# Class scales by one-hot products in four row tiles of the TensorE array, and issued ahead of single token tiles

## The chip, the cores and the metric

The kernel runs on one core of one Trainium2 chip. Its time is the device time of one execution in microseconds (us), as the median of several executions. The engines are TensorE (PE, matrix products), VectorE (DVE, element-wise work), ScalarE (ACT, activations and copies), GpSimd (POOL, indirect loads and a few element-wise steps) and SyncE (SP, which issues the plain DMAs of this kernel in one queue, in order). "PEld" in the profile is TensorE's loading of weights.

## The reference

The reference works on x of shape 2 x 2048 x 512, that is 4096 tokens of 512 channels. A modulated linear layer, a gated linear recurrence and a gated MLP come first, and their result is added to x. What the change touches is the part after these. There, each token is normalised and scaled and shifted by rows that its class ids choose:

```python
h = _ln(x, pw_g[pathway_ids], pw_b[pathway_ids])        # 500 classes
h = _ln(h, cp_g[compartment_ids], cp_b[compartment_ids])  # 5 classes
t = _ln(x, tm_g[time_steps], tm_b[time_steps])            # 5 classes
s = _ln(x, ms_g[scale_type], ms_b[scale_type])            # 2 of 3 classes
cat = concatenate([w0*h, w1*t, w2*m, w3*n, w4*r, w5*s])   # m, n, r: x plus a vector
y = _ln(silu(cat @ int_W1 + int_b1) @ int_W2 + int_b2, int_g, int_be)
```

y is then quantised to int8 for each token, multiplied with a quantised 512 x 512 matrix, and added to x. Inputs and outputs are float32.

## The kernel before, in words

The first stages (the modulated layer, the recurrence, the two up-projections of the MLP) run over four spans of 1024 tokens. They are followed by the down-projection `down`, also over four spans, whose products `dn_a`, `dn_b` and `dn_d` read four operands b11, b12, b21 and b22 (tiles `op`), loaded from a DRAM scratch (line 701, `op<-pp_d`). A product is made by a scheme of seven smaller products ("steps") of sums and differences of these four (line 200 makes the sums on DVE). The dictionary `early` hangs small pieces of preparation behind these steps; in the first span they are the loading of the class tables (`load_classes`, lines 921 and 922), the making of one-hot rows (`one_hots`, line 899), the splitting of each class table into three bf16 parts (`split`, `class_gains`, lines 908 to 911), and loads of state weights (`load_state`, line 59). A later piece loads `rhsT` (line 59).

The last stage, the token stage, runs over eight blocks of 512 tokens, each as four token tiles of 128. For block i+1:

- `by_tokens` transposes x to tokens, normalises it, and gathers the pathway rows. It also transposes the one-hot rows of the four token tiles (line 1182, tile `tr_oh`), and ACT copies the result into `oh` (line 1186): 30 rows by 512 tokens.
- `by_channels` transposes the normalised tokens back to channels (line 1133) as `lnT` and `hT`; ACT copies them out (line 1136).
- `gains` multiplies them by the class scales. A scale for 128 channels and 512 tokens is one bf16 product of a 30-row table (10 classes in three bf16 parts) with the 30 one-hot rows (line 1224). Three tables (n = 0, 1, 2) and four groups of 128 channels make twelve products per block, in six pairs. Each pair fills one PSUM tile of two banks, named `gain`, out of two such tiles that all `tr` users share, and one DVE multiply (line 1228) consumes it, giving `tT`, `lnT` or `hT`.
- `up` is the first MLP product (`ps_h`, line 130), on block i, with `by_tokens` and `by_channels` of block i+1 and the int8 product of block i-1 as pieces among its steps. `added` (line 1264) adds the class shifts (table 3) in it.
- `down2` is the second MLP product of block i (`ps_o`, line 1300), one 512-wide product for each token tile, followed by a DVE addition (line 1304) and the statistics of the last norm (line 1110). It takes the token tiles in the order 2, 3, 0, 1.

A tile framework puts the instructions of each engine in an order of its own, from priorities and dependencies; the program above gives the data flow and a first order. In the order that it built, the six pairs of gains of block i+1 stand among the first products of `down2` of block i, two gains and then one ps_o product.

Of the kernel before, what the change touches and what calls it, by code (L numbers as in the profile page):

```python
# [9 lines left out]
FP = mybir.dt.float32  # L10
# [19 lines left out]
G = 32  # L30
# [20 lines left out]
def adaln_attn_ffn(ctx: ExitStack, tc: tile.TileContext, a: dict, out: bass.AP):  # L51
# [235 lines left out]


    groups = ident.rearrange("p (j r) -> p j r", r=G)
    sums = const.tile([P, G], FP, name="sums")  # L290
    nc.vector.tensor_reduce(sums, groups.rearrange("p j r -> p r j"), AX.X, ALU.add)
    apart = const.tile([P, 3, B], FP, name="apart")
    nc.vector.tensor_copy(apart, groups[:, 0:3, 0:B])
    nc.vector.tensor_add(apart[:, 0, :], groups[:, 0, 0:B], groups[:, 3, 0:B])
# [39 lines left out]
        wsq.append(t)  # L334
    rows_k = tp.tile([P, T], FP, tag="k", name="ps_dcoef_k")
    rows_of("ps_dcoef", [(st2[:, c, :], wsq[c]) for c in range(C)], rows_k)
    ps = columns_of("ps_dcoef", rows_k, sums[:, 0:B])
    dflat = dcoef.rearrange("p c b -> p (c b)")
    dv = small.tile([P, 2, C * B], FP, name="dv")
    nc.vector.tensor_scalar(  # L340
# [328 lines left out]


    R = 10
    onehot = w3.tile([P, NT, 3, R], BF, name="onehot", bufs=1)
    tables = w3.tile([3 * R, 4, D], BF, name="tables", bufs=1)
    idx_pw = w3.tile([P, NT], mybir.dt.int32, name="idx_pw", bufs=1)
    betas = w3.tile([P, 3, C, R], FP, name="betas", bufs=1)
    dn = ph1.enter_context(ExitStack())
# [131 lines left out]
    def state_columns(m):  # L808
        name = ("mem", "noi", "res")[m]
        v = vs[m]  # L810
        ps = columns_of(f"ps_sv_{m}", held[m][:, C, :], sums[:, 0:B])
        for o in range(C):
            nc.vector.tensor_scalar(
                v[:, o, :], ps[:, o, :], col(f"L0_cond2_{name}_b2", o), None, ALU.add
            )
# [67 lines left out]
    def one_hots():  # L883

        nc.sync.dma_start(idx_pw, a["idx_pw"])
        row_of = small.tile([P, R], FP, name="row_of")
        for k in range(R):
            nc.vector.memset(row_of[:, k : k + 1], float(k - (0 if k < 5 else 5 if k < 8 else 8)))
        ids = small.tile([P, 3, NT], FP, name="ids")
        for k, n in enumerate(("idx_c", "idx_m")):  # L890
            raw = small.tile([P, NT], mybir.dt.int32, tag="raw", name=n)
            nc.sync.dma_start(raw, a[n])
            nc.vector.tensor_copy(ids[:, k, :], raw)
        nc.vector.memset(ids[:, 2, : NT // 2], 0.0)
        nc.vector.memset(ids[:, 2, NT // 2 :], 1.0)
        for k, (lo, hi) in enumerate(((0, 5), (5, 8), (8, 10))):
            shape = [P, NT, hi - lo]
            for n in range(3):
                nc.vector.tensor_tensor(
                    onehot[:, :, n, lo:hi],  # L900
                    ids[:, k, :].unsqueeze(2).to_broadcast(shape),
                    row_of[:, lo:hi].unsqueeze(1).to_broadcast(shape), ALU.is_equal,
                )

    def split(k, t, parts, engine=nc.vector):

        for n, h in enumerate(parts):
            ins = engine.tensor_copy(h, t)
            if n < 2:
                engine.tensor_sub(t, t, h)  # L910
            nc.sync.dma_start(tables[n * R : n * R + R, k, :], h)
        return ins

    TABLES = (("tm", 0, 5), ("ms", 5, 3), ("cp", 0, 5))
# [189 lines left out]
    def tr(name, dtype=FP):  # L1104
        turn[0] ^= 1
        return tr_ps[turn[0]].tile([P, 2, D], dtype, tag="tr", name=name)
# [34 lines left out]
    def block(tag, i=None):  # L1141
        return place(tag if i is None else f"{tag}{i % 2}", C, T)
# [15 lines left out]
    def by_tokens(i, k, behind=()):  # L1158


        def queued(n):
            return tc.issue_after(behind[n].ins) if behind else nullcontext()

        x2n = k["x2n"] = place(f"x2n{i % 2}", J, D)
        mv = small.tile([P, J, 2], FP, tag="mv", name=f"mv1_{i}", bufs=4)
        for q in PAIRS:
            if behind:
                turn[0] = 1
            with queued(q):
                pt = tr(f"tr_x_{i}_{q}")  # L1170
                for j in (0, 1):
                    for c in range(C):
                        nc.tensor.transpose(
                            pt[:, j, ts(c, P)], k["x2T"][:, c, ts(2 * q + j, P)], ident
                        )
            nc.scalar.copy(duo(x2n, q), pt)
            for j in (2 * q, 2 * q + 1):
                stats(mv, j, x2n[:, j, :], f"s1_{i}")
        with queued(2):
            po = tr(f"tr_oh_{i}", BF)[: 3 * R].rearrange("r a b -> r (a b)")[:, :T]  # L1180
            for j in range(J):
                nc.tensor.transpose(
                    po[:, ts(j, P)], onehot[:, i * J + j].rearrange("p n r -> p (n r)"), identb
                )
        k["oh"] = place(f"oh{i % 2}", T, dtype=BF)[: 3 * R]
        nc.scalar.copy(k["oh"], po)
        r = rstd_of(mv, f"r1_{i}")

        h0 = k["h0"] = []
        mv2 = small.tile([P, J, 2], FP, tag="mv", name=f"mv2_{i}", bufs=4)  # L1190

        ln = k["ln"] = [place(f"o4_{q}", 2, D) for q in PAIRS]
        for q in PAIRS:
            pw = place(f"pw{q}", 2, 2 * D)
            h0.append(pw[:, :, 0:D])
            for j in (0, 1):
                gather(i * J + 2 * q + j, pw[:, j, :])
                normed(ln[q][:, j, :], x2n[:, 2 * q + j, :], mv, r, 2 * q + j)
            nc.vector.tensor_mul(h0[q], ln[q], h0[q])
            nc.vector.tensor_add(h0[q], h0[q], pw[:, :, D : 2 * D])  # L1200
            for j in (0, 1):
                stats(mv2, 2 * q + j, h0[q][:, j, :], f"s2_{i}")
        r = rstd_of(mv2, f"r2_{i}")
        for j in range(J):
            t = h0[j // 2][:, j % 2, :]
            last = normed(t, t, mv2, r, j)
        return last
# [5 lines left out]
        for q in PAIRS:  # L1213
            to_channels(hT, q, k["h0"][q], f"tr_h_{i}_{q}")

    def gains(i, k):

        tT = k["tT"] = block("tT")
        lnT, hT = k["lnT"], k["hT"]
        for n, dst, src in ((0, tT, lnT), (1, lnT, lnT), (2, hT, hT)):  # L1220
            for q in PAIRS:
                ps = tr(f"gain_{i}_{n}_{q}")
                for c in (0, 1):
                    nc.tensor.matmul(
                        ps[:, c, :], tables[:, n, ts(2 * q + c, P)], k["oh"],
                        start=True, stop=True,
                    )
                nc.vector.tensor_mul(duo(dst, q), ps, duo(src, q))

    h1s, o4s, mvs = {}, {}, {}  # L1230

# [2 lines left out]
    def up(i, k, then):  # L1234
# [25 lines left out]
        def added(n, ps):  # L1260

            o, half = {1: (0, h_a), 2: (0, h_b), 3: (2, h_b), 4: (2, h_a)}[n]
            for u in (0, 1):
                nc.tensor.matmul(
                    ps[u], tables[:, 3, ts(o + u, P)], k["oh"][:, half],
                    start=False, stop=(n != 2), skip_group_check=True,
                )

# [19 lines left out]
            banks, tap, out11, out12, out21, out22, then, added, True,  # L1288
        )

    def down2(i, then=()):

        h1 = h1s.pop(i)
        o4 = o4s[i] = [place(f"o4_{q}", 2, D) for q in PAIRS]
        mv = mvs[i] = small.tile([P, J, 2], FP, tag="mv", name=f"mv3_{i}", bufs=4)
        for q in (1, 0):
            for j in (2 * q, 2 * q + 1):
                ps = m2_ps.tile([P, D], FP, tag="mm", name=f"ps_o_{i}_{j}")
                for c in range(C):
                    nc.tensor.matmul(  # L1300
                        ps, h1[:, c, ts(j, P)], w2[:, c, :], start=(c == 0), stop=(c == C - 1)
                    )
                t = o4[q][:, j % 2, :]
                nc.vector.tensor_add(t, ps, b2_bc)
                stats(mv, j, t, f"s3_{i}")
            if q in then:
                then[q]()
# [57 lines left out]
    pb = m2_ps.tile([P, D], FP, tag="mm", name="ps_bias")[:R]  # L1365
    pc = m2_ps.tile([P, D], FP, tag="mm", name="ps_bias_s")[:R]
    n = 0
    nc.tensor.matmul(pb, sums[:, 0:R], bias, start=True, stop=False)
    for m, at in ((0, 0), (2, 2)):
        for c in range(C):  # L1370
            nc.tensor.matmul(
# [15 lines left out]
        nc.vector.tensor_sub(bias[:, 2 * P :], bias[:, 2 * P :], pc[:, 2 * P :])  # L1387
        tables_done = split(3, bias, [place(f"tab{n % 2}", D, dtype=BF)[:R] for n in range(3)], nc.gpsimd)
    by_channels(0, k)
    gains(0, k)  # L1390
    last = None
    for i in range(NB):
        nxt = load(i + 1) if i + 1 < NB else None
        then = {}
        if last:
            qs = []
            then[0] = lambda: qs.append(last_norm(i - 1))
            then[2] = lambda: int8_product(i - 1, qs[0], last["x2n"])
        if nxt:
            then[3] = lambda: by_tokens(i + 1, nxt)  # L1400
            then[6] = lambda: by_channels(i + 1, nxt)
        up(i, k, then)
        if nxt:
            gains(i + 1, nxt)
            down2(i)
        else:
            qs = {}

            def norm_of(q):
                qs[q] = last_norm(i, (q,))  # L1410
            down2(i, {1: lambda: norm_of(1)})
            int8_product(i, qs[1], k["x2n"], (1,))
            norm_of(0)
            int8_product(i, qs[0], k["x2n"], (0,))
        last, k = k, nxt
# [68 lines left out]
```

## The time and the profile before

| | us |
|---|---|
| median of 3 executions | 2105.15 |
| lowest and highest | 2104.56, 2105.45 |
| the profiled execution | 2105.82 |
| its span in the trace | 2104.0 |
| one block of the token stage, first gain to first gain | 78.95 |

Over the span PE is busy for 97%, DVE for 58%, ACT for 33% and POOL for 7%. The trace has a line for every instruction: start, length, engine, line of the program, operation, output and inputs, the size of the operands, and what ended an idle time before it. In such rows "x2" is a count of like instructions in a row, and the length goes from the first start to the last end. A product in float32 shows as two passes. Starts and ends are in us from the start of the span.

### The profile page before, as it was taken

The numbers are of one execution on the slowest core, as the hardware profiler recorded it, in microseconds if no ns is written. First come the engines' busy times: TensorE is split into PE (matmuls) and PEld (weight loads), VectorE is DVE, ScalarE is ACT, GpSimd is POOL, SyncE is SP. The second block draws the span as 40 slices with busy tenths as digits, with TensorE's granted clock in tenths as the row PEclk, the third lists the DMA queues.
The fourth block names the chain that finished last, engine by engine and source line by source line (L and its number), as shares of the span: only waits on it lengthen the run. The fifth ranks groups of instructions, "written<-read, shape, count | busy, mean of one in ns | idle before, by whom it ended". The sixth has DMA issues, their size and how long they took to land.

```text
span 2104.0 us, 16699 instructions
## 1 busy us (share of the span) xinstructions
PE 2048.2 (97%) x6230; PEld 1075.1 (51%) x6238; DVE 1213.3 (58%) x1788; ACT 691.5 (33%) x894; POOL 155.6 (7%) x125
## 2 busy tenths in 40 slices
PE   8989999999899999999999999999999999999996
PEld 4334444443344444444444444435776776776773
DVE  6875655565732433324335465486587787787765
ACT  3557787877542222222221000001312312312300
POOL 1240000001200000000000000072000000000000
PEclk9999999999999999999999999999999999999998
DMA  5672212132311212211235846624101201201000
GB/s 203 252 253 73 80 40 80 40 100 80 120 40 50 80 40 72 79 40 50 95 105 185 296 138 206 224 86 156 61 20 61 81 21 61 81 21 60 21 20 20
DMA packets 85071, 199.52 MB, mean 95 GB/s; under 512 B 6407, under 2 KB 34303, under 8 KB 80893
## 3 DMA queue, kind: packets, MB, share of 16 engines
q1 hardware_dynamic: 80380, 181.67, 25.1%
q0 software_dynamic: 4608, 16.78, 2.4%
q8 instruction: 49, 0.80, 0.2%
q14 instruction: 34, 0.27, 0.0%
HBM read 131.18 MB, written 67.13 MB: 94 GB/s over the span
## 4 chain that ended last, share of the span: by engine, by line
PE 85%; DVE 6%; ACT 6%; DMA 1%; issue 1%; SPq 0%; DVEq 0%; ACTq 0%
PE up_a L130 16%; PE ps_h_a L130 11%; PE up_d L130 8%; PE dn_a L130 7%; PE ps_o L1300 5%; PE ps_h_d L130 5%; PE rec_a L130 5%; PE up_b L130 4%; PE dn_d L130 4%; PE rec_d L130 4%; PE ps_h_b L130 3%; PE y_a L130 2%; PE rec_b L130 2%; PE dn_b L130 1%; PE ps_f L1347 1%
## 5 line engine op out<-in xcount | busy, mean ns | idle before, releaser
L130 PE MATMUL up_a<-h,w_up 128*128 128x512 f32 x384 | 172.8, 592 | 0.0
L130 PE MATMUL up_a<-h2T,w_up 128*128 128x512 f32 x384 | 172.6, 592 | 0.0
L130 PE MATMUL dn_a<-op,w_dn 128*128 128x512 f32 x384 | 167.4, 594 | 0.0
L623 DVE SCALAR_TENSOR_TENSOR prod<-up_d,cols,k 128x512 f32<-128x512 f32 x48 | 35.9, 751 | 198.4 <-ACT k L256 198.4
L256 ACT COPY k<-up_a 128x512 f32<-128x512 f32 x144 | 84.3, 585 | 197.7 <-PE up_a L130 197.6
L603 ACT ACTIVATE gate<-gate,cols 128x512 f32<-128x512 f32 x96 | 68.8, 721 | 213.4 <-DVE gate L602 213.4
L130 PE MATMUL rec_a<-hT,w_rec 128*128 128x512 f32 x256 | 116.7, 596 | 5.2 <-ACT k L256 5.2
L1300 PE MATMUL ps_o<-int_w,h 128*128 128x512 f32 x256 | 121.6, 610 | 0.0
L130 PEld LDWEIGHTS up_a<-h2T,w_up 128*128 128x128 f32 x384 | 73.0, 190 | 91.8 <-issue 91.8
L130 PEld LDWEIGHTS up_a<-h,w_up 128*128 128x128 f32 x384 | 72.9, 190 | 91.9 <-issue 89.4
L130 PE MATMUL rec_a<-h,w_rec 128*128 128x512 f32 x256 | 117.0, 596 | 1.6 <-ACT k L256 1.3
L130 PEld LDWEIGHTS dn_a<-op,w_dn 128*128 128x128 f32 x384 | 72.2, 190 | 88.8 <-issue 86.7
L130 PE MATMUL up_d<-h,w_up 128*128 128x512 f32 x192 | 86.4, 593 | 0.8 <-DVE prod L623 0.8
L130 PE MATMUL up_d<-h2T,w_up 128*128 128x512 f32 x192 | 87.0, 592 | 0.0
L130 PE MATMUL up_b<-h,w_up 128*128 128x512 f32 x192 | 86.3, 592 | 0.0
L130 PE MATMUL dn_d<-op,w_dn 128*128 128x512 f32 x192 | 84.2, 595 | 0.0
L130 PEld LDWEIGHTS rec_a<-hT,w_rec 128*128 128x128 f32 x256 | 47.9, 190 | 69.2 <-issue 55.0
L130 PEld LDWEIGHTS rec_a<-h,w_rec 128*128 128x128 f32 x256 | 48.7, 191 | 64.8 <-issue 59.7
L602 DVE TENSOR_TENSOR gate<-up_b,k 128x512 f32<-128x512 f32 x48 | 32.8, 690 | 73.1 <-PE up_b L130 72.1
L1300 PEld LDWEIGHTS ps_o<-int_w,h 128*128 128x128 f32 x256 | 45.0, 189 | 58.4 <-issue 58.4
L256 ACT COPY k<-rec_a 128x512 f32<-128x512 f32 x96 | 53.8, 580 | 51.7 <-PE rec_a L130 51.6
L130 PE MATMUL rec_d<-h,w_rec 128*128 128x512 f32 x128 | 60.6, 617 | 6.8 <-DVE i L534 5.3
(372 smaller groups left out, 3472.5 us busy)
## 6 DMA issues: line engine op xcount, KB each, us to landing
pp_d<-prod SPq DMA_DIRECT2D x48, 512.0 KB
op<-pp_d SPq DMA_DIRECT2D x16, 1536.0 KB
x<-in_xT SPq DMA_DIRECT2D x4, 2048.0 KB
y_d<-y SPq DMA_DIRECT2D x16, 512.0 KB
h_d<-y SPq DMA_DIRECT2D x16, 512.0 KB
h<-h_d SPq DMA_DIRECT2D x4, 2048.0 KB
yr<-y_d SPq DMA_DIRECT2D x16, 512.0 KB
hs_d<-yr SPq DMA_DIRECT2D x16, 512.0 KB
```

Of the source, the lines that this page charges most:

```text
L130: ins = nc.tensor.matmul(ps, ws[k // 2][:, slot, k % 2, ts(u, P)], xs[k], start=(first and k == 0), stop=(last and k == n - 1), skip_group ...
L256: nc.scalar.copy(t, ps)
L602: nc.vector.tensor_add(gate[u][:, half], ps, kept)
L603: nc.scalar.activation(gate[u][:, half], gate[u][:, half], AF.Gelu, bias=col("L0_attn_mlp_gate_b", fs[u]),)
L623: nc.vector.scalar_tensor_tensor(prod[u][:, b_], ps, col("L0_attn_mlp_fc_b", fs[u]), kept, ALU.add, ALU.add)
L1300: nc.tensor.matmul(ps, h1[:, c, ts(j, P)], w2[:, c, :], start=(c == 0), stop=(c == C - 1))
L1347: nc.tensor.matmul(ps, qT[:, j, ts(c, P)], rq[:, c, :], start=(c == 0), stop=(c == C - 1))
```

## The change

The one-hot rows get 32 columns instead of 30 (the two more are zero), and four copies of them are made by transposing each token tile four times, into partitions 0, 32, 64 and 96 of the PSUM tile. The three scale tables are likewise stored four times, at partitions 0, 32, 64 and 96; the table of shifts (number 3) is stored once. The four products of one table then read four different groups of 32 partitions, one for each group of 128 channels, and write four different PSUM banks. `gains` handles one table (n) for each call, and the calls for block i+1 stand in `down2` of block i, ahead of the token tiles 2, 3 and 0, instead of ahead of all of `down2`. One tile `ids` has a single buffer, and a tile is renamed (`sums` to `summing`), without other effect.

```diff
-    onehot = w3.tile([P, NT, 3, R], BF, name="onehot", bufs=1)
-    tables = w3.tile([3 * R, 4, D], BF, name="tables", bufs=1)
+    onehot = w3.tile([P, NT, G], BF, name="onehot", bufs=1)
+    tables = w3.tile([P, 4, D], BF, name="tables", bufs=1)
...
+        nc.gpsimd.memset(onehot, 0.0)
...
-                    onehot[:, :, n, lo:hi],
+                    onehot[:, :, n * R + lo : n * R + hi],
...
-            nc.sync.dma_start(tables[n * R : n * R + R, k, :], h)
+            for g in range(4 if k < 3 else 1):
+                nc.sync.dma_start(tables[G * g + n * R : G * g + n * R + R, k, :], h)
...
-            po = tr(f"tr_oh_{i}", BF)[: 3 * R].rearrange("r a b -> r (a b)")[:, :T]
+            po = tr(f"tr_oh_{i}", BF).rearrange("r a b -> r (a b)")[:, :T]
             for j in range(J):
-                nc.tensor.transpose(
-                    po[:, ts(j, P)], onehot[:, i * J + j].rearrange("p n r -> p (n r)"), identb
-                )
-        k["oh"] = place(f"oh{i % 2}", T, dtype=BF)[: 3 * R]
+                for g in range(4):
+                    nc.tensor.transpose(po[ts(g, G), ts(j, P)], onehot[:, i * J + j], identb)
+        k["oh"] = place(f"oh{i % 2}", T, dtype=BF)
...
-    def gains(i, k):
-
-        tT = k["tT"] = block("tT")
+    def gains(i, k, n):
         lnT, hT = k["lnT"], k["hT"]
-        for n, dst, src in ((0, tT, lnT), (1, lnT, lnT), (2, hT, hT)):
-            for q in PAIRS:
-                ps = tr(f"gain_{i}_{n}_{q}")
-                for c in (0, 1):
-                    nc.tensor.matmul(
-                        ps[:, c, :], tables[:, n, ts(2 * q + c, P)], k["oh"],
-                        start=True, stop=True,
-                    )
-                nc.vector.tensor_mul(duo(dst, q), ps, duo(src, q))
+        if n == 0:
+            k["tT"] = block("tT")
+        dst, src = ((k["tT"], lnT), (lnT, lnT), (hT, hT))[n]
+        ps = [tr(f"gain_{i}_{n}_{q}") for q in PAIRS]
+        for c in range(C):
+            of = slice(G * c, G * c + 3 * R)
+            nc.tensor.matmul(
+                ps[c // 2][:, c % 2, :], tables[of, n, ts(c, P)], k["oh"][of],
+                start=True, stop=True,
+            )
+        for q in PAIRS:
+            nc.vector.tensor_mul(duo(dst, q), ps[q], duo(src, q))
...
-    def down2(i, then=()):
+    def down2(i, nxt=None, then=()):
...
             for j in (2 * q, 2 * q + 1):
+                if nxt and j in (2, 3, 0):
+                    gains(i + 1, nxt, (2, 3, 0).index(j))
                 ps = m2_ps.tile([P, D], FP, tag="mm", name=f"ps_o_{i}_{j}")
...
-    gains(0, k)
+    for n in range(3):
+        gains(0, k, n)
...
-            gains(i + 1, nxt)
-            down2(i)
+            down2(i, nxt)
```

Here P is 128, G is 32, R is 10, C and J are 4, D and T are 512, and NT is 32, the number of token tiles.

More of the change, by code (lines that the diff above doesn't have):

```diff
@@ L289, in adaln_attn_ffn @@
     groups = ident.rearrange("p (j r) -> p j r", r=G)
-    sums = const.tile([P, G], FP, name="sums")
-    nc.vector.tensor_reduce(sums, groups.rearrange("p j r -> p r j"), AX.X, ALU.add)
+    summing = const.tile([P, G], FP, name="sums")
+    nc.vector.tensor_reduce(summing, groups.rearrange("p j r -> p r j"), AX.X, ALU.add)
     apart = const.tile([P, 3, B], FP, name="apart")
@@ L336, in adaln_attn_ffn @@
     rows_of("ps_dcoef", [(st2[:, c, :], wsq[c]) for c in range(C)], rows_k)
-    ps = columns_of("ps_dcoef", rows_k, sums[:, 0:B])
+    ps = columns_of("ps_dcoef", rows_k, summing[:, 0:B])
     dflat = dcoef.rearrange("p c b -> p (c b)")
@@ L810, in state_columns @@
         v = vs[m]
-        ps = columns_of(f"ps_sv_{m}", held[m][:, C, :], sums[:, 0:B])
+        ps = columns_of(f"ps_sv_{m}", held[m][:, C, :], summing[:, 0:B])
         for o in range(C):
@@ L888, in one_hots @@
             nc.vector.memset(row_of[:, k : k + 1], float(k - (0 if k < 5 else 5 if k < 8 else 8)))
-        ids = small.tile([P, 3, NT], FP, name="ids")
+        ids = small.tile([P, 3, NT], FP, name="ids", bufs=1)
         for k, n in enumerate(("idx_c", "idx_m")):
@@ L1264, in added @@
                 nc.tensor.matmul(
-                    ps[u], tables[:, 3, ts(o + u, P)], k["oh"][:, half],
+                    ps[u], tables[: 3 * R, 3, ts(o + u, P)], k["oh"][: 3 * R, half],
                     start=False, stop=(n != 2), skip_group_check=True,
@@ L1367, in adaln_attn_ffn @@
     n = 0
-    nc.tensor.matmul(pb, sums[:, 0:R], bias, start=True, stop=False)
+    nc.tensor.matmul(pb, summing[:, 0:R], bias, start=True, stop=False)
     for m, at in ((0, 0), (2, 2)):
@@ L1410, in norm_of @@
                 qs[q] = last_norm(i, (q,))
-            down2(i, {1: lambda: norm_of(1)})
+            down2(i, None, {1: lambda: norm_of(1)})
             int8_product(i, qs[1], k["x2n"], (1,))
```

## The prediction

> **What bounds the kernel now.** I read the page's busy line first, then windows, timeline and tile views of the token stage, then waits. The profiled execution took 2105.82 us (span 2104.0, clock 0.992), 0.67 above the median 2105.15; sums are made against it, and 0.67 comes off at the end. A measurement of this kernel can tell about 0.2% (4.2 us) from no change.
>
> ```profile
> PE 2048.2 (97%) x6230; PEld 1075.1 (51%) x6238; DVE 1213.3 (58%) x1788; ACT 691.5 (33%) x894; POOL 155.6 (7%) x125
> ...
> 1593.54:1672.49 78.95, 78.82 (x360) 56.78 (x360) 59.53 (x99) 16.64 (x24) 3.76 (x5) 1.00 0.15 54
> ```
>
> The second line is one token block, gain to gain: 78.95 us, TensorE (PE) busy 78.82, VectorE (DVE) 59.53. So PE sets a block, and what leaves PE's row leaves the block. The PE timeline where the change acts:
>
> ```profile
> 1593.54 0.60 PE L1224 MATMUL gain<-zone_C,tables 30*128 30x512 bf16 x2
> 1594.07 1.13 PE L1300 MATMUL ps_o<-int_w,h 128*128 128x512 f32 x2
> 1595.13 0.60 PE L1224 MATMUL gain<-zone_C,tables 30*128 30x512 bf16 x2
> 1595.66 1.12 PE L1300 MATMUL ps_o<-int_w,h 128*128 128x512 f32 x2
> ...
> 1601.48 0.60 PE L1224 MATMUL gain<-zone_C,tables 30*128 30x512 bf16 x2
> 1602.02 9.71 PE L1300 MATMUL ps_o<-int_w,h 128*128 128x512 f32 x22
> ```
>
> Columns: start, length, instructions. Six pairs of gains, 1.59 us apart (1595.13 − 1593.54), each followed by two passes of ps_o. A pass alone takes (9.71 − 0.59)/21 = 0.434, with 0.59 the length of a single one. So **one pair costs PE 1.59 − 2 × 0.43 = 0.73 us**. The single starts in the trace divide it: 0.226 between the two gains, and about 0.50 that a pair pays however many gains it has: 0.304 from its last gain to ps_o, 0.105 extra on the next pass (0.534 for 0.429), 0.09 extra before the next pair.
>
> [...] column tiles run together:
>
> ```profile
> 1166.78 1.06 PE L301 MATMUL ps_sh_r<-state_w 128*32 128x512 f32 x8
> ```
>
> Eight 512-column passes in 1.06 us; one by one they would need 8 × 0.43 = 3.4. Row tiles do not occur before. [...] Four gains at 0.226 are 0.90[...]; perfect overlap gives 0.23. [...] the change's four outputs go to the two banks each of two tr tiles.
>
> **The change, part by part.**
>
> *Gains of blocks 1 to 7.* The built order has, where six pairs stood: pair, one ps_o, pair, three ps_o, four gains (n=1), four ps_o, four gains (n=2), eight ps_o. Two gains that overlap cost 0.73 − 0.22 = 0.51; four cost 0.50 + 0.02 = 0.52[...]. Before 6 × 0.73 = 4.38; after 2 × 0.51 + 2 × 0.52 = 2.06. **−2.3 per block, −16.1 in seven**[...].
>
> *Block 0* keeps six groups, each now overlapping: 6 × 0.2 = **−1.2** (bounds −0.3, if waits for DVE's multiplies fill the room, to −1.3).
>
> *Do the products come in time?* A gain waits for its tr tile. Before, DVE multiplies (1.22 each) follow gains 1.59 apart; now PE is at group three 0.51 + 0.86 + 0.51 + 2.58 = 4.46 after the first, at group four 4.46 + 0.52 + 3.44 = 8.42. ACT's second hT copy ends at 1594.65, 1.11 after the first gain, ahead of the second pair (1.37). Group three needs the tT products, done near 3.3. Group four needs both lnT products; DVE's built order puts a ps_o add and a bn_stats among them. From the last pass of tile 2, 4.65 + 0.59 + 1.15 + 0.7 + 1.22 = 8.3 (starts of such rows in DVE's timeline). Slack of 0.1 only, and 0.5 late is the bound, 3.5 in seven blocks: I take **+0.5** in all.
>
> *Transposes of the one-hot rows*, 4 to 16 per block.
>
> ```profile
> 1568.81 0.40 PE L1182 MATMUL tr_oh<-identb,onehot 128*30 128x128 bf16 x4
> 1569.14 0.70 PE L130 MATMUL ps_h_a<-tT,w_int 128*128 128x256 f32 x2
> ```
>
> Four cost 0.33 to the next start, 0.055 apart. Twelve more, in column tiles like ps_sh_r's, add about 0.05; one by one 12 × 0.055 = 0.66. **+0.4** in eight blocks (0 to +5.3). The ACT copy goes from 30 to 128 partitions with the same 512 elements each, so its 0.57 stays, under an ACT busy 16.6 of 79.
>
> *Table copies.* Nine DMA issues of SP become 36.
>
> ```profile
> L911 SPq DMA_DIRECT2D tables<-classes x9: 722/743/835, 1154.8 to 1176.9; - x9
> ```
>
> 27 × 0.743 = 20 us on SP, between 1155 and 1197 us in the down stage. Behind them wait loads of op and the state weights; behind DVE's 4 us of waits on such landings (three, now on four copies each) stand taps and operand sums. I walked the built SP order with the old times: op b11 leaves about 4 us later (1174), b12 about 1191, and b21, which PE reads next, at 1202.2, since its buffer is read by PE until 1200.7 and SP had idle room till then.
>
> ```profile
> 1202.04 0.61 SPq L701 DMA_DIRECT2D op<-pp_d  x1
> ...
> PE dn_b L130 <- DMA op<-pp_d: 1.4, 1, 1.4
> ```
>
> This b21 load is the one PE waits for (1.4). Two 1 MB loads, state_w and rhsT, issued at 1186.85 and 1197.86, now stand behind it in SP's order, so it shares the DMA engines with less: **−0.7** (between −1.4 and +2). On DVE the operand sum op_21 (1163.2) has one of the longer waits ahead of it, and the taps that follow wait for PE themselves until 1179, 1184 and 1195, up to 2 us each: covered. rhsT, later by about 10, is reduced ahead of a sum that PE needs at 1247, ready near 1237.
>
> *Rest.* The memset of onehot on POOL (a 128x1024 f32 one takes 0.95) falls at 1128, where POOL is otherwise idle, before DVE's is_equal; DVE's next big sum waits for PE till 1136: nothing. Renamed tiles, table 3 and the two `added` products: as before.
>
> Sum: −16.1 − 1.2 + 0.5 + 0.4 − 0.7 = −17.1; 2105.8 − 17.1 = 2088.7 profiled, less 0.67: **2088.0**.
>
> **The rivals.**
>
> *A. Row tiles run one after another.* For it: the trace before shows column tiles only. Against it: the independence shown there[...]. Pairs keep 0.73, fours cost 0.50 + 3 × 0.226 = 1.18: 3.82 for 4.38, −0.56 × 7 = −3.9; block 0 nothing. With transposes in a row (+5.3) and −0.7: 2105.15 + 0.7 = about **2106**, with quick transposes 2101: no change that can be told.
>
> *B. DVE is late at the last four* by its bound, 0.5 in seven blocks: 2088 + 3 = **2091**. Speaks for it: slack 0.1. Against: no wait beyond DVE's own row.
>
> *C. Slower: SP's queue becomes the wait.* If SP had no idle room ahead of b21, its issue would come 20 us late, and PE would stand in the dn_b row for as much. Some copies also wait for DVE, which overwrites their source only once the fourth copy has landed, 3 × 0.74 = 2.2 after the first. Without relief the rest of the sum is −16.4: 2105.15 − 16.4 + 20 + 2.2 = **2111**. It decides once b21 leaves over 16.4 us later than at 1202. For it: 27 copies in front. Against it: the queue's rows between 1155 and 1202 sum to 19 of 47 us, so 20 more can be held, and b21 waits for PE anyway.
>
> **How the numbers follow.** Forecast 0.80 (with sizes from 2085.5 to 2091), B 0.09, A or half of it 0.06, C 0.03, other 0.02. Lower end: 2105.15 − 16.1 − 1.3 − 1.4 = 2086.3[...]: 2085. Upper end: B, serial transposes (+4.9) and no relief (+0.7) give 2096.6: 2096.5. Faster takes forecast, B and a little of A; same the rest of A and a C half held; slower the remainder of C.
>
> **What would show it.** Right: the block period falls from 78.95 to about 76.7 with PE still over 99% busy; L1228 gains in groups of two, two, four, four, with starts within 0.02 us; 16 transposes in under 0.45; no PE wait on a product lnT. Wrong: gains 0.22 apart in a group (A); a PE wait ahead of the last group (B); a longer wait in the row dn_b from op (C), or DVE taps late after 1161; a period that falls with a gap between groups above 0.55.

## The result, and the profile after

The change makes the kernel faster by 0.9%: 2085.93 us (2084.65 to 2088.27) against 2105.3 us, a ratio of 0.9909 with a 95% interval of 0.9891 to 0.9926. The forecast was 2088.0. A second set of runs gave 2088.38 and 0.9913 (0.9898 to 0.9928). The profiled execution after took 2084.65 us, with a span of 2082.9.

One block of the token stage, first gain to first gain, in the windows view of after (period, then busy time and instructions of PE, PEld, DVE, ACT, POOL):

```profile
1586.13:1662.79 76.66, 76.58 (x375) 56.70 (x374) 59.03 (x99) 16.66 (x24) 3.75 (x5) 1.00 0.16 56
```

The period falls from 78.95 to 76.66, that is by 2.29, and PE is still busy for 99.9% of it. The PE timeline of after, at the place that was shown of before:

```profile
1586.13 0.39 PE L1228 MATMUL gain<-zone_C,tables 30*128 30x512 bf16 x2
1586.44 1.12 PE L1308 MATMUL ps_o<-int_w,h 128*128 128x512 f32 x2
1587.50 0.39 PE L1228 MATMUL gain<-zone_C,tables 30*128 30x512 bf16 x2
1587.82 2.84 PE L1308 MATMUL ps_o<-int_w,h 128*128 128x512 f32 x6
1590.59 0.40 PE L1228 MATMUL gain<-zone_C,tables 30*128 30x512 bf16 x4
1590.92 3.70 PE L1308 MATMUL ps_o<-int_w,h 128*128 128x512 f32 x8
1594.55 0.39 PE L1228 MATMUL gain<-zone_C,tables 30*128 30x512 bf16 x4
```

A row of four gains takes 0.40, as long as a row of two (0.39), and hardly longer than one gain (0.384 in the tile view): the four run together. Their single starts in the trace are 3 to 4 ns apart. The distance to the next ps_o is 0.32 for two and 0.33 for four.

DVE's rows ahead of the last group show how near the products came to being late (start, length, in brackets the idle time before and what ended it):

```profile
1590.70 0.69 DVE L1312 TENSOR_TENSOR zone_C<-ps_o,rows 128x512 f32<-128x512 f32 x1 [1.54 <-PE ps_o L1308]
1591.31 1.21 DVE L1233 TENSOR_TENSOR lnT<-gain,lnT 128x1024 f32<-128x1024 f32 x1
1592.44 0.68 DVE L1113 BATCH_NORM_STATS2 s_st<-zone_C 128x6 f32<-128x512 f32 x1
1593.04 1.21 DVE L1233 TENSOR_TENSOR lnT<-gain,lnT 128x1024 f32<-128x1024 f32 x1
```

The second lnT product ends at 1594.25, and the last group starts at 1594.55 without a wait: a slack of 0.3.

The transposes of the one-hot rows, sixteen instead of four:

```profile
1434.43 0.41 PE L1186 MATMUL tr_oh<-identb,onehot 128*32 128x128 bf16 x16
1434.76 0.66 PE L1136 MATMUL tr_l<-ident,zone_A 128*128 128x128 f32 x4
```

They take 0.33 to the next start, as four did before (unrounded, 0.01 more). The table copies and the wait behind them (the tile view, then the waits):

```profile
L914 SPq DMA_DIRECT2D tables<-classes x36: 706/708/1478, 1151.6 to 1193.2; - x36
...
  DVE classes L910: 10.3, 3
```

```profile
PE dn_b L130 <- DMA op<-pp_d: 0.5, 1, 0.5
```

DVE waits 10.3 us for landings in place of 4.0, and PE's wait for b21 is 0.5 in place of 1.4.

The two traces differ by 2104.0 − 2082.9 = 21.1 us. From the first gain to the end it is 649.05 before and 632.16 after, −16.9. The other 4.2 lie ahead of the first gain, and 2.7 of them ahead of the recurrence, in a part that the change does not touch. The experiments show where most of these 4.2 come from.

### The profile page after: what moved, and what is told of

Same layout as the page of the kernel before. It is cut to its first block, busy times and chain, and to the rows that moved or that the text cites. A ratio compares the mean times of both kernels' runs of the same rounds, so it can differ in the third digit from the quotient of the medians.

```text
span 2082.9 us, 16921 instructions
## 1 busy us (share of the span) xinstructions
PE 2029.6 (97%) x6334; PEld 1072.6 (51%) x6334; DVE 1208.1 (58%) x1788; ACT 691.3 (33%) x894; POOL 154.1 (7%) x126
## 4 chain that ended last, share of the span: by engine, by line
PE 82%; DVE 7%; ACT 6%; DMA 3%; issue 1%; SPq 1%; DVEq 0%; ACTq 0%
PE up_a L130 16%; PE ps_h_a L130 11%; PE up_d L130 8%; PE ps_h_d L130 5%; PE ps_o L1308 5%; PE rec_a L130 5%; PE dn_a L130 5%; PE up_b L130 4%; PE rec_d L130 4%; PE dn_d L130 3%; PE ps_h_b L130 3%; PE y_a L130 2%; PE rec_b L130 2%; PE ps_f L1355 2%; PE y_d L130 1%
```

## The experiments

The theory, from the prediction: a group of gains costs PE g = 0.51 us however many run together in it, and each gain on rows that are already in use adds s = 0.22. (A row tile is here one of the four groups of 32 partitions of the change, used by a product on 30 rows; a serial step is a gain that follows another on the same rows.) The rivals were that tiling alone or placement alone carries the gain, and that the copies cost something that a larger gain hides.

### The change once more

Edit: none.

> The changed kernel once more, unedited, as the base for the other kernels here and for the scatter of the start. In its first profile y_a, the first product of the first stage, stood 2.3 us earlier than in the profile of before, ahead of anything that the change touches. Theory: this is scatter between executions (how long the first products run at half pace); then it moves again here by about 1 to 2 us and the time is 2085 to 2088. Rival: the change itself brings it (its program is laid out differently); then y_a starts again near 18.6 us for its second half, as in the first profile after.

Measured: 2088.38 us (ratio 0.9913), span 2086.6. Period and token stage are those of the first profile (76.66; 632.16 from the first gain to the end). The start is not. The timelines of PE's second product of the first stage, here and in the first profile after:

```profile
21.17 3.60 PE L130 MATMUL y_b<-x,w_cond 128*128 128x512 f32 x8
```

```profile
18.61 3.60 PE L130 MATMUL y_b<-x,w_cond 128*128 128x512 f32 x8
```

In some executions the first products run at half pace for longer (starts 0.85 apart in place of 0.43). In the twelve profiles y_b starts between 18.6 and 22.6, and two profiles of one kernel lie 2.6 apart here and 2.2 for the kernel before. The start is scatter, not the change.

### Placement alone

```diff
-            for g in range(4 if k < 3 else 1):
+            for g in range(1):
...
-                for g in range(4):
+                for g in range(1):
...
-            of = slice(G * c, G * c + 3 * R)
+            of = slice(0, 3 * R)
```

> Placement alone: gains called ahead of token tiles 2, 3 and 0 as in the change, but all on one group of 32 partitions, with one copy of tables and one-hot rows. Theory (a group costs 0.50 us however many gains it has, and gains on the same rows cost 0.226 each): groups of 2, 2, 4, 4, that is 2 x 0.73 + 2 x 1.18 = 3.82 for 4.38 us per block, -0.56 x 7 = -3.9 against before, nothing in block 0 or in the down stage: 2101.4. Rival, that the saving is the placement's: close to 2089, the change's own time. Rival, that DVE becomes late at the last group since four products in a row delay it: 2103 to 2105.

Measured: 2100.93 us, ratio 0.9978 (0.9967 to 0.9988).

```profile
1593.43:1671.78 78.35, 78.27 (x361) 57.11 (x361) 59.03 (x99) 16.63 (x24) 3.74 (x5) 1.00 0.16 54
```

The period is 78.35, −0.60 where −0.56 was expected. Four gains of one group on one set of rows stand at 0.96 to the next ps_o, where four in row tiles take 0.33. Placement alone is a quarter of the change's 2.29.

### Row tiles alone

```diff
-                if nxt and j in (2, 3, 0):
-                    gains(i + 1, nxt, (2, 3, 0).index(j))
...
-            down2(i, nxt)
+            for n in range(3):
+                gains(i + 1, nxt, n)
+            down2(i)
```

> Row tiles alone: tables and one-hot rows in four groups as in the change, but all gains of a block ahead of down2, as before. Theory: six groups of two that overlap, 0.51 for 0.73 us: -0.22 x 6 x 8 blocks = -10.6, and -0.9 in the down stage: 2105.3 - 11.5 = 2093.8. Rival, that DVE's multiplies (1.22 us for each pair) hold PE once groups stand 1.37 apart, with a 1.22 multiply and additions between: half of it, 2099. Rival, that tiling brings nothing by itself: 2104.

Measured: 2093.81 us, ratio 0.9946 (0.9933 to 0.9960).

```profile
1589.09:1666.78 77.69, 77.61 (x374) 56.71 (x374) 59.43 (x99) 16.66 (x24) 3.75 (x5) 1.00 0.15 55
```

−1.26 per block where −1.32 was expected; DVE holds nothing up. The periods now give both prices twice: two groups less (77.69 to 76.66) are 1.03, so g = 0.515; six serial steps less (78.95 to 77.69) are 1.26, so s = 0.21; and placement alone, with the change's four groups and eight serial steps, is 76.66 + 8 × 0.21 = 78.34, for 78.35 measured. Neither part alone is the gain: tiles give 1.26, merging groups gives 0.60 without tiles and 1.03 with them.

### The preparation alone

```diff
-            of = slice(G * c, G * c + 3 * R)
+            of = slice(0, 3 * R)
...
-                if nxt and j in (2, 3, 0):
-                    gains(i + 1, nxt, (2, 3, 0).index(j))
...
-            down2(i, nxt)
+            for n in range(3):
+                gains(i + 1, nxt, n)
+            down2(i)
```

> The cost of the change's preparation without its use: 36 table copies, 16 transposes per block, a 128-row copy of them, but all gains read the first group of partitions and stand ahead of down2 as before. Theory: the block period stays 78.95, the 16 transposes take 0.33 us as the four did, SP's copies delay the b21 load by about 0.8 us and not PE by more than 1 us: 2104 to 2105.5, the time of before. Rival (the slower case of the prediction in a small form): the copies cost 3 us or more, which the change pays back out of a larger gain: 2108 or more.

Measured: 2103.33 us against 2103.3, ratio 1.0000 (0.9992 to 1.0008), period 78.96. The preparation costs nothing that this measurement tells. In its trace PE waits 1.06 for the b21 load:

```profile
1208.85 3.67 PE L130 MATMUL dn_b<-op,w_dn 128*128 128x512 f32 x8 [1.06 <-DMA op<-pp_d]
```

### The kernel before once more

Edit: none.

> The kernel before once more, unedited, for the two places where its profile and the first profile after differ ahead of the token stage: the start (first y_a product) and the wait of 1.43 us in dn_b for op from pp_d. Theory: both are scatter of single executions; y_a's second half starts near 21.1 us here (the slow start, seen in four of five other profiles by now in one form or another) and the dn_b wait lies between 0 and 1.4. Rival: the 1.43 us belongs to the kernel before, since state_w and rhsT stand ahead of the load that is waited for; then it is 1.3 to 1.5 again, the load taking 10.5 us from issue to the first product that reads it.

Measured: 2104.87 against 2103.3 us, ratio 1.0003 (0.9995 to 1.0011). Its y_b starts at 18.84, the early kind. And b21 is there in time:

```profile
1194.57 14.76 PE L130 MATMUL dn_a<-op,w_dn 128*128 128x512 f32 x34
1209.33 3.24 PE L130 MATMUL dn_b<-op,w_dn 128*128 128x512 f32 x7
```

No idle time stands before dn_b. So the 1.43 us on which a term of the prediction rested does not belong to the kernel but to that one transfer: from issue to the first product that reads it, b21 took 10.6 in the first profile of before and no more than 9.1 here, in the same order of SP.

### Table copies on POOL's queue

```diff
-                nc.sync.dma_start(tables[...], h)
+                (nc.sync if g == 0 else nc.gpsimd).dma_start(tables[...], h)
```

> The change with the 27 additional table copies issued by POOL's queue; the order of SP's queue is then that of before, with state_w and rhsT ahead of the b21 load. Theory by the prediction's step (two loads of 1 MB ahead of b21 lengthen its landing): b21 again takes 10.5 us from issue to first product and the dn_b wait is 1.4, so 0.9 slower in that place than the first profile after. Rival, from the run with placement alone, where the order of SP was that of before and no wait showed: under 0.5 us, b21 landing within 9 us. The median is that of the change, 2086 to 2088, either way.

Measured: 2093.07 us, ratio 0.9949 (0.9936 to 0.9962). The time missed both expectations: by the ratios it gives back some 8 of the change's 18 to 19 us. The wait at b21 is 1.0, and b21 is read 10.1 after its issue, nearer to the theory (1.4 and 10.5) than to the rival; but the trace puts this wait down to a step of DVE, and the whole stage has moved, so it does not decide between them. The token stage is that of the change (period 76.67). The loss is in the down stage, on PE and then on DVE:

```profile
1176.78 0.95 PE L310 MATMUL ps_sh_c<-apart,state_w 128*128 128x6 f32 x8
1181.29 1.94 PE L130 MATMUL dn_a<-op,w_dn 128*128 128x512 f32 x2 [3.55 <-DVE dk L731]
```

```profile
1169.98 0.41 DVE L910 CAST classes<-classes 10x512 bf16<-10x512 f32 x1 [0.29 <-DMA tables<-classes]
1178.34 0.41 DVE L910 CAST classes<-classes 10x512 bf16<-10x512 f32 x1 [7.95 <-DMA tables<-classes]
1178.79 0.68 DVE L912 TENSOR_TENSOR classes<-classes 10x512 f32<-10x512 f32 x1
1179.50 0.41 DVE L910 CAST classes<-classes 10x512 bf16<-10x512 f32 x1
1179.95 0.68 DVE L912 TENSOR_TENSOR classes<-classes 10x512 f32<-10x512 f32 x1
1180.56 0.67 DVE L731 TENSOR_TENSOR dk<-dn_a,res 128x512 f32<-128x512 f32 x1
```

DVE reuses the buffer that the copies read, so its next cast (L910) waits 7.95 us for copies to land: POOL issues the last ones ahead of it from 1169.27 to 1172.55, and the cast starts at 1178.34, 5.8 later. The tap of dn_a (the DVE step that reads it, L731) stands behind it, and the PE step that overwrites dn_a waits 3.55 for the tap. Here the wait cost more than its own length: the passes after it are slow at first (the row of two takes 1.94, where 1.02 is usual), and the whole row of 24 takes 12.26, where the same row takes 10.55 in the profile after. The slow passes are another 1.7. In all, the way from the stage's first product to the first gain takes 334.6, for 328.0 and 328.6 in the two profiles of the change. What follows moves with it: b21 is issued 82.6 us after the stage's first product instead of 77.4.

This is the part of the slower rival C that spoke of DVE; the other part, a full SP queue, did not occur. In the change DVE waits for such landings too, 10.3 us in all, but there the tap stands ahead of the longest of these waits and ends 5.1 before the PE step that needs it. Why they land so late is not shown.

### What a group pays

```diff
-            for g in range(4 if k < 3 else 1):
+            for g in range(1):
...
+        nc.gpsimd.memset(tables, 0.0)
...
-                ps[c // 2][:, c % 2, :], tables[of, n, ts(c, P)], k["oh"][of],
+                ps[c // 2][:, c % 2, :], tables[:, n, ts(c, P)], k["oh"],
```

> What the 0.50 us of a group is: placement as in the change, all gains on one table copy in rows 0 to 29 of a 128-row table that is zero elsewhere, multiplied as full 128-row products (no row tile), one after another. Groups of 2, 2, 4, 4 with 8 serial steps of 0.21, as in the run with placement alone (period 78.35). Theory, that the 0.50 is the switch between a 32-row tile and the full array: it falls to 0.23 (the first gain of a group's own pass) and less than 0.1 more, 4 x 0.2 to 0.3 less per block: a period near 77.3, 2093. Rival, that it is the switch between bf16 and float32 passes or a wait for weights: the period stays 78.3, 2101.

Measured: 2088.47 us, ratio 0.9926 (0.9913 to 0.9939), period 77.17.

```profile
1592.14 0.59 PE L1228 MATMUL gain<-zone_C,tables 128*128 128x512 bf16 x2
1592.57 1.02 PE L1308 MATMUL ps_o<-int_w,h 128*128 128x512 f32 x2
1593.43 0.59 PE L1228 MATMUL gain<-zone_C,tables 128*128 128x512 bf16 x2
```

Two full-row gains take 0.43 to the next ps_o, and two passes of ps_o then 0.86: twice 0.216 and twice 0.43, with nothing for the change of data type. The window holds 12 × 0.216 = 2.59 for the gains, which leaves 77.17 − 2.59 = 74.58 for the rest; the tiled kernel leaves 76.66 − 4 × 0.515 = 74.60. So **0.30 of the 0.51 is the switch into and out of a 32-row tile**, and the kernel before paid it six times a block.

The weight loads show where the 0.30 lies. Here is the load for a group of gains, first in the change, then in full rows:

```profile
1590.59 0.10 PEld L1228 LDWEIGHTS <-tables 30*128 30x128 bf16 x4 [0.76 <-issue]
```

```profile
1593.00 0.10 PEld L1228 LDWEIGHTS <-tables 128*128 128x128 bf16 x1 [0.24 <-issue]
```

In full rows the weights are loaded 0.43 ahead of their product (1593.43), during the pass before. In the row tile they are loaded in the instant in which the products start (1590.59), after 0.76 without a load, and those of the next ps_o in the instant in which it starts (1590.92). The excess over the full-row passes is 0.10 ahead of the group, 0.10 behind it and 0.10 on the second pass of ps_o. Full rows in the change's placement, with no row tile in the gains, reach 78.95 − 77.17 = 1.78 of the 2.29.

### A later placement, and two versions from these findings

```diff
-                if nxt and j in (2, 3, 0):
-                    gains(i + 1, nxt, (2, 3, 0).index(j))
+                if nxt and j in (3, 0, 1):
+                    gains(i + 1, nxt, (3, 0, 1).index(j))
```

> The change with its three calls one token tile later, ahead of tiles 3, 0 and 1: the second tr tile is then free at the first call, so that there are three groups of four in place of 2, 2, 4, 4. Theory (0.51 us per group): -0.51 x 7 = -3.6 against the change, 2082.4 if the change is 2086. Rival: the last products (hT) come later relative to the next block's second step, which reads them, or push last_norm back on DVE; PE then waits in ps_h_b and the gain is lost: 2086 to 2090.

Measured: 2084.93 us, ratio 0.9902 (0.9886 to 0.9917), against the change's 2088.38 in the same set. The period is 76.16, −0.50: three groups of four, and no wait for the products.

The second version adds full-row `added` products:

```diff
+        nc.gpsimd.memset(tables[:, 3, :], 0.0)
...
-                    ps[u], tables[: 3 * R, 3, ts(o + u, P)], k["oh"][: 3 * R, half],
+                    ps[u], tables[:, 3, ts(o + u, P)], k["oh"][:, half],
```

> The later placement (calls ahead of tiles 3, 0 and 1), and the `added` products (table 3, two per step, four times in a block) as full 128-row products on a table that is zero outside rows 0 to 29, with no row tile. Theory from the runs before: a switch to row tiles and back costs 0.30 us beyond the passes (4 groups and 8 serial steps: 78.35 in row tiles, 77.17 in full rows), so four `added` pairs save 4 x 0.30 = 1.2 per block: period 76.15 - 1.2 = 74.95, and -1.2 x 8 = -9.6 in all: about 2075.5 where the later placement alone is 2085. Rival: an `added` pair hides its switch in the float32 passes around it, so that nothing is saved: 2085.

Measured: 2078.83 us, ratio 0.9869 (0.9854 to 0.9885), period 75.60: faster than both kernels. But `added` gave 0.56 per block and not 1.2. Start by start against the version with the later placement, the four pairs save 0.29, 0.29, 0.24 and 0.10, together 0.91. Of this 0.39 is lost again, 0.13, 0.17 and 0.09, at three places where PE now comes too early: its weight loads start 0.04 after ACT, DVE and ACT have finished reading a PSUM tile. The first and the last in the view of the weight loads (in brackets is the idle time of the loads, not PE's loss):

```profile
1626.58 0.30 PEld L130 LDWEIGHTS ps_h_d<-zone_A,w_int 128*128 128x128 f32 x2 [0.27 <-ACT zone_B L1256]
1663.44 0.53 PEld L1137 LDWEIGHTS tr_h<-ident,pw 128*128 128x128 f32 x5 [0.29 <-ACT lnT L1140]
```

In the version with the later placement PE reaches these rows later, behind the switch, and the same reads cost it nothing or less. Five blocks compared in this way agree within 0.01.

The third has no row tile in gains and `added`: the full-row kernel above with both edits of this section.

> No row tiles at all in gains and `added`: one table copy padded with zeros to 128 rows, full-row products, calls ahead of tiles 3, 0 and 1. Theory: each of the twelve gains costs its pass of 0.213 and a group nothing more, however many there are: 12 x 0.213 = 2.56 for three groups of four in row tiles at 0.515, so 1.0 slower per block than the version with tiles and full-row `added`: period near 75.96, 2083 to 2084. Rival, that a group without a tile switch still pays 0.1 to 0.3: slower than 2085.

Measured: 2083.25 us, ratio 0.9905 (0.9890 to 0.9921), period 76.61. It is 1.01 per block slower than the version with tiled gains; 12 × 0.216 for 3 × 0.515 gives 1.05. The period itself is 0.65 above the expected one, since it has the same `added` products.

## Why the prediction was right, point by point

- **The gains of blocks 1 to 7** were the whole of it and were sized right: −2.3 per block forecast, −2.29 measured, from overlap (s = 0.21) and fewer groups (g = 0.515). That row tiles overlap fully, which the trace before could not show, is shown: four gains stand at 0.96 to the next row on the same rows and at 0.33 in row tiles, a ratio of 2.9.
- **The 0.50 us per group**: the trace before showed the sum and not its cause. 0.30 of it is gone in full rows and so belongs to the change between a row tile and full rows. The other 0.20 was the first gain's own pass (0.216 in full rows).
- **Block 0**, forecast −1.2: first gain of block 0 to that of block 1 went from 59.63 to 58.72, −0.9. The prediction kept six groups, but block 0 had five: its second and third pair stood together before, and the order of after puts a product between them. With s = 0.21 and one switch of 0.30 more, −1.26 + 0.30 gives −0.96.
- **Products in time**, forecast +0.5: nothing; the slack was 0.3 and not 0.1. Rival B did not occur.
- **Transposes**, forecast +0.4: 0.01 per block, 0.1 in all. The column tiles overlap: sixteen transposes take 0.33 to the next start, as four did. The ACT copy behind them takes 0.61 for 128 partitions, and took 0.57 for 30.
- **The table copies, forecast −0.7: this step failed, in sign.** It took one wait of 1.43 in one execution for a property of the order of SP's queue. The repeated kernel before has no such wait, and in the other three profiles with nine copies on SP no wait at that place is above 0.2; of the six with all 36 copies on SP five wait 0.3 to 1.1 and one does not wait. That b21 then shares the DMA engines with less was an estimate; they are busy for 0.91 of the 11 us from 1202 on in before and for 0.97 of those from 1200 on in the profile after. With state_w and rhsT behind it, b21 does not come much sooner: where PE waited for it, it came 8.6 to 9.2 after its issue, and with the two loads ahead of it 10.4 in the first profile of before and 9.1 in the kernel without row tiles. But the copies send b21 0.3 to 1.2 us later than in the order of before (76.8 to 77.7 after the stage's first product, for 76.55), where +0.2 was worked out. In the profile after, SP's last waits ahead of b21 are for landings, 2.6 of them for the op load before it, which was itself issued 3.1 later than before (67.18 for 64.08).
- **The sum** came out because the misses are small against their opposites: −17.3 for the gains of all blocks, and −16.9 measured from the first gain to the end. The measured −19.4 of the first set and −15.8 of the second lie on both sides; the start of single executions moves by up to 4 us. That the forecast of 2088.0 lies within 2.1 of both medians is in part luck.
- Rival A (row tiles one after another) is refuted. Rival C did not occur in the change, but what it says of DVE was the right thing to fear: one choice of queue away, it takes back some 8 us.

## What to carry to other kernels

When an engine is full, price what a group of small products pays for being a group: here the switch into a row tile (0.30) was dearer than a product (0.21), and fewer, fuller groups (1.03 per block) or full rows padded with zeros (1.18) were worth nearly as much as the overlap (1.26). Before a term rests on one wait of one execution, look whether a second execution has it. Copies that read a buffer hold up the engine that refills it (DVE for 7.95 us with POOL's queue); look at what stands behind that refill, not only at the queue that carries them. And when PE gets shorter, look for copies whose end it now has to wait for: they took back 0.39 of the 0.91 in `added`.

## What the runs showed of the hardware that was not expected

- Between full-row products, two gains on 30 rows take 0.53 to the next row in the kernel before, and two padded to 128 rows 0.43. In the change the weights of a group on 30 rows are loaded in the instant in which its products start (1590.59), and in full rows 0.43 ahead of them (1593.00 for 1593.43).
- In full rows, bf16 gains and float32 products follow each other with no gap (0.43 for two bf16 passes, then 0.43 for each float32 pass).
- Sixteen bf16 transposes in four column tiles take only 0.01 longer to the next start than four in one (0.33).
- The first products of an execution run at half pace for a varying time (0.85 apart in place of 0.43): the second product of the first stage starts between 18.6 and 22.6 us in the twelve profiles, in no relation to the kernel.
- With the table copies on POOL's queue, slow passes followed a wait of PE: after its 3.55, two passes took 1.94 in place of 1.02.
